# Graph attention on one core: another order of products in the first pair of tiles of a batch, and the mean's product one step later

## The chip, the cores and the metric

The kernel runs on one core of a Trainium2 chip. The metric is the device time of one execution in microseconds, the median of three runs. PE is the matrix engine, DVE the vector engine, ACT the scalar engine; POOL issues the indirect DMAs (gathers) and a few small operations, SP the plain DMAs.

## The reference, cut to what matters

`x` has 16 batches of 1024 nodes with 512 features, `adj` is one sparse 0/1 matrix of 1024 x 1024 for all batches, and there are 8 heads of 64.

```python
q = (x @ Wq + bq).reshape(b, n, H, HD)
k = (x @ Wk + bk).reshape(b, n, H, HD)
v = (x @ Wv + bv).reshape(b, n, H, HD)
scores = jnp.einsum('bqhd,bkhd->bhqk', q, k) / jnp.sqrt(jnp.float32(HD))
scores = scores + (1.0 - adj)[None, None, :, :] * -1000000000.0
attn = jax.nn.softmax(scores, axis=-1)
out = jnp.einsum('bhqk,bkhd->bqhd', attn, v).reshape(b, n, d)
return _layernorm(x + out @ Wo + bo)
```

## The kernel before

Nodes are ranked by their number of neighbours and cut into 8 tiles of 128 queries. The attention of a tile isn't a dense product: for each query, the rows k | v of its neighbours are fetched by gathers, one *block* at a time (a block is one neighbour for each of 128 queries). There are 530 blocks in all, 32 to 34 for a batch. A query without neighbours gets the average of all v, so each batch also needs that average as one more row of the table of k | v rows.

**The loop of steps.** The program is written out by one loop (L1485), with a step n for each block. A step puts into DVE's program the product q·k of block n + 4 (L1263), the sum of earlier blocks (L1307) and the scores (L1267); into ACT's the exponentials and the weighting of v (L1291); into POOL's the gathers of block n + 8. What earlier steps put off with `later(k, fn)` comes behind that (L1519), k steps after the call. Last come *units* of work for PE, out of two lists: `finishing` (the four products of an output tile with Wo, L1075) goes ahead of `fronts`. A step has a credit, a share of the work that is left, and hands out units as long as the credit is above zero; each unit takes its cost off (0.86 for a product, 0.44 for the transposes of one tile, 0.88 for the lone product). What a step hasn't used is carried over. If the next unit isn't ready yet, the loop breaks off. Functions on the list `urgent` are called behind the first unit of a step.

**The fronts** make q, k and v for all tiles, a pair of tiles (b, j) at a time, j from 0 to 3, as far as two batches ahead of the attention. For k and v together, a scheme with seven half-size products in place of eight is used (L984 to L996). Each unit holds two code products, which are four matmul instructions (a float32 product takes two). In its names, x and z are two fixed PSUM banks, used twice by each pair:

- x1 writes bank x; ACT copies it to e (L960); x2 adds to the same bank and may be handed out only when that copy is in the program. Then out_k copies the bank to k.
- p6 takes s2 as input, and DVE makes w out of it (L963); p7 takes s3, and DVE makes g (L966).
- z1 takes s1 and writes bank z; out_v1 on DVE (L975) makes v of the second tile out of it. z2 takes s4, adds to the same bank, may be handed out only when out_v1 is in the program, and waits for it on the chip. out_v0 (L979) follows z2.
- p4 makes k of the second tile (out_k1, L970).
- q0 and q1 are the products for q of the two tiles (L790), where they are needed.
- xt0 and xt1 transpose the two x tiles of the *next* pair (L748). One step later ACT copies the result (L752); one step after the second copy, `combine` (L774 to L777) makes s1 to s4 for the next pair on DVE. s1, s2 and s3 have one buffer each, s4 has two.

A unit of the seven is ready only when its pair's s1 to s4 are in the program:

```python
return [(2 * PRODUCT, pe, lambda: (need is None or need in R) and (b, j) in SX and bool(combined))]
```

In a first pair (j = 0) of a batch from 2 on, tile 1 needs no q, so q1 is empty. Tile 0 of an even and the following odd batch are treated together: in an even batch q0 is empty, in an odd one it is four products and the *lone product* (L881, in bf16), whose squares are summed on ACT (L889).

**The mean.** When both tiles of the last pair (j = 3) are sent, `add_v` (L854) adds their v to a running sum one step later, and one step behind that `mean_pe` (L856) is put on the urgent list: a product with a column of 1/1024 (L858). A step later ACT copies it (L862), SP stores it as the last row of the batch's table (L864), and `set_up[b]` is set. The gathers of the batch's blocks are only put into the program once that is set (L1504).

Of the kernel before, what the change touches and what calls it, by code (L numbers as in the profile page):

```python
# [177 lines left out]
def kernel(  # L178
# [75 lines left out]
    with ExitStack() as main:  # L254
# [6 lines left out]
        def fill_psum(name):  # L261
            return psum.tile([P, HALF], F32, tag="fill", name=name, bufs=4)
# [67 lines left out]
        def kv_of(b):  # L330

            if b < PAIRED_FROM:
                return solo_rows[b], 0
            rows = pair_views[b // 2 % 2][b % 2]
            return (rows, N + 1) if b % 2 else (rows[0:N + 1, :], 0)
# [104 lines left out]
        now, plan, rest, urgent, known, waiting, combined = [0], {}, {}, [], [], [], []  # L440

        def later(k, fn):
            plan.setdefault(now[0] + k, []).append(fn)
# [340 lines left out]
        def product(name, lhs, w, out):  # L784

            def unit(c):
                if c == 0:
                    PS[name] = fill_psum(name)
                p = PS[name]
                nc.tensor.matmul(p, lhs(c), w[:, c, :], start=(c == 0), stop=(c == NPAIR - 1))  # L790
                if c == NPAIR - 1:
                    del PS[name]
                    later(1, lambda: out(p))

            return [(PRODUCT, lambda c=c: unit(c), None) for c in range(NPAIR)]
# [11 lines left out]
        def pair(b, j):  # L807
# [8 lines left out]
            def out_q(i, p):  # L816

                assert gathered[0] >= start[max(0, b - ROWS + 1)]
                tag, bufs = ("q", 2) if b or j else ("y", Y_BUFS)
                q = work.tile([P, D], F32, tag=tag, name=f"q_{b}_{tt[i]}", bufs=bufs)  # L820
                nc.vector.scalar_tensor_tensor(q, p, scale, bq_bc, op0=OP.mult, op1=OP.add)
                later(1, lambda: nc.sync.dma_start(q_rows[b % ROWS][ds(tt[i] * P, P), :], q))

            def out_k(i, p):
                kv = new_kv(i)
                nc.scalar.copy(kv[:, 0:D], p)
                later_last(1, lambda: norm(b, tt[i], kv[:, 0:D]))

            def out_v(i, p):
                nc.scalar.copy(KV[b, tt[i]][:, D:], p)  # L830
                send(i)

            def send(i):
                assert b < PAIRED_FROM or gathered[0] >= start[max(0, b // 2 * 2 - 2)]
                kv = KV[b, tt[i]]
                rows, base = kv_of(b)
                for lo, hi in ((0, LONE), (LONE + P, 2 * P)) if b and tt[i] == 0 else ((tt[i] * P - (LONE if b and tt[i] == 1 else 0), None),):
                    hi = lo + P if hi is None else hi
                    part = slice(0 if lo % P == 0 or hi - lo == P else LONE, P if hi - lo == P or lo else LONE)
                    later(1, lambda lo=lo, hi=hi, part=part: nc.sync.dma_start(rows[base + lo:base + hi, :], kv[part, :]))  # L840
                R["sent"] = R.get("sent", 0) + 1
                if R["sent"] == 2:
                    later(1, add_v)
                    if j == NT // 2 - 1:
                        later(2, lambda: urgent.append(mean_pe))

            def add_v():
                kv = [KV.pop((b, t))[:, D:] for t in tt]
# [49 lines left out]
            def lhs(i):  # L898
                return lambda c: XT[b, tt[i]][:, ts(c, P)]

            q0, q1 = (
                product(f"pq_{b}_{tt[i]}", lhs(i), W["q"], lambda p, i=i: out_q(i, p)) if b == 0 or tt[i] != ONE_KEY else []
                for i in range(2)
            )
            if j == 0 and b >= PAIRED_FROM:
                q0 = []
                if merged(b):
                    q0 = product(f"pq_{b}_0", lambda c: BOTH[b // 2][:, 1, c, :], W["q"], lambda p: out_q(0, p))
                    q0 += lone_product()
            n = b * NT + 2 * j + 2  # L910
            xt = [u for t in (n, n + 1) if t < B * NT for u in transpose_x(t // NT, t % NT)]
# [24 lines left out]
            def a(i, h):  # L936
                return XT[b, tt[i]][:, ts(h, HD2)]

            def unit(bank, left, right, first, after, need):
                def pe():  # L940
                    if first:
                        R[bank] = fill_psum(f"p{bank}_{b}_{j}") if bank[0] == "p" else psum.tile(
                            [P, HALF], F32, tag=bank, name=f"{bank}_{b}_{j}", bufs=1
                        )
                    l = left()
                    for c in range(2):
                        nc.tensor.matmul(  # L947
                            R[bank], l[:, ts(c, P)], right[:, c, :], start=(first and c == 0), stop=(c == 1),
                            skip_group_check=True,
                        )  # L950
                    later(1, after)

                return [(2 * PRODUCT, pe, lambda: (need is None or need in R) and (b, j) in SX and bool(combined))]
# [14 lines left out]
            def out_k1():  # L968
                kv = KV[b, tt[1]]
                nc.vector.tensor_tensor(kv[:, 0:D], R["p4"], R["g"], op=OP.add)  # L970
                send(1)
                later_last(1, lambda: norm(b, tt[1], kv[:, 0:D]))
# [5 lines left out]
            def out_v0():  # L978
                nc.vector.tensor_tensor(KV[b, tt[0]][:, D:], R["z"], R["w"], op=OP.add)  # L979
                send(0)  # L980

            def s(i):
                return lambda: SX[b, j][i - 1]

            units = []
            units += unit("x", lambda: a(0, 0), B11, True, out_e, None)
            units += unit("p6", s(2), T2, True, out_w, None)
            units += q0
            units += unit("x", lambda: a(0, 1), B21, False, lambda: out_k(0, R["x"]), "e")
            units += unit("p7", s(3), T3, True, out_g, None)  # L990
# [472 lines left out]
        with tc.manual_schedule():  # L1463
# [3 lines left out]
            for b in range(B):  # L1467
                for j in range(NT // 2):
                    fronts += pair(b, j)
                fronts_by.append(sum(u[0] for u in fronts))  # L1470
# [14 lines left out]
            while n < total or plan or rest or urgent or done or finishing or spilled or lone_tiles or not guarded:  # L1485
# [6 lines left out]
                elif n in start:  # L1492

                    b = start.index(n)
# [110 lines left out]
```

## Time and profile before

| what | value |
|---|---|
| runs shown | 1876.87, 1874.72, 1875.09 us; median 1875.09 |
| profiled execution | 1894.52 us, of which the span of the profile is 1892.4 us |
| busy, of the span | PE 96%, DVE 90%, ACT 82%, POOL 67% |
| matmul instructions | 5149 |
| granted PE clock, mean | 0.990 |
| HBM traffic | 298 GB/s over the span |

A line of the busy table gives an engine's busy time, its share of the span and its instructions. A line of the groups gives code line, engine, operation, output and input tiles, shapes and count; then busy time and mean of one in ns; then the idle time of the engine just before the instructions and what ended most of it. A line of the waits gives who waited for whom, us in total, the number of times and the longest. A line of the timeline gives start, duration (a merged group's), engine, code line, operation, tiles, shapes and count, and in brackets idle time and its releaser; "issue" stands for a wait that the profile can't name. In the table of windows the columns are the stretch, its length, busy time and count of PE, PEld, DVE, ACT and POOL, the granted clock, the share of the DMA engines and GB/s.

### The profile page before, as it was taken

How to read it: one execution, taken by the hardware profiler on the slowest of the kernel's cores; microseconds unless marked ns; L12 is line 12 of the kernel's file. 1: busy time of each engine (PE TensorE's matmuls, PEld its weight loads, DVE VectorE, ACT ScalarE, POOL GpSimd, SP SyncE). 2: the span in 40 equal slices, each digit the busy share in tenths (PEclk: the TensorE clock that was granted, in tenths of full speed). 3: DMA queues.
4: the chain of work that ended last, by engine and by line, in shares of the span. 5: the costliest groups of instructions: out<-in, count | busy, mean ns of one | idle time of the engine just before them, and what ended most of it. 6: DMA issues, size and time to landing. Idle time of an engine off the chain costs nothing. (4 is left out here: it accounts for less than half of the span.)

```text
span 1892.4 us, 25171 instructions
## 1 busy us (share of the span) xinstructions
PE 1816.5 (96%) x5149; PEld 876.6 (46%) x5149; DVE 1695.3 (90%) x3470; ACT 1557.4 (82%) x6128; POOL 1262.6 (67%) x1189
## 2 busy tenths in 40 slices
PE   7979999999999999999999999999999999999996
PEld 3434444444545454444444444444545444444442
DVE  6888879999998999899999989899999989997875
ACT  3627868988888988988898878988899989977885
POOL 1366765777676776767676766767676866656884
PEclk9989999999999999999999999999999999999998
DMA  7356786888989897989889897989889899989993
GB/s 279 115 167 215 226 290 229 309 298 291 322 266 319 303 333 256 345 290 310 299 284 329 279 324 261 334 303 309 286 302 352 297 332 319 329 282 319 340 332 137
DMA packets 188149, 544.63 MB, mean 288 GB/s; under 512 B 32602, under 2 KB 32622, under 8 KB 187986
## 3 DMA queue, kind: packets, MB, share of 16 engines
q0 software_dynamic: 116400, 382.82, 60.4%
q1 hardware_dynamic: 68510, 154.30, 21.7%
q10 hardware_dynamic: 3076, 5.82, 0.8%
q14 instruction: 120, 0.98, 0.2%
q8 instruction: 43, 0.70, 0.2%
HBM read 419.52 MB, written 144.34 MB: 298 GB/s over the span
## 5 line engine op out<-in xcount | busy, mean ns | idle before, releaser
L1291 ACT ACTIVATE pv<-kvg,pv 128x64 f32<-128x64 f32 x3544 | 893.4, 340 | 1.8 <-issue 1.8
L1242 POOL DMA_INDIRECT kvg<-kv_pair,place_row x462 | 522.6, 1131 | 258.6 <-issue 94.5
L790 PE MATMUL po<-wo,oT 128*128 128x512 f32 x816 | 379.2, 600 | 2.0 <-DVE vsum L854 1.2
L790 PE MATMUL pq<-wq,xT 128*128 128x512 f32 x792 | 369.4, 598 | 1.3 <-DVE s L1267 0.8
L1267 DVE TENSOR_REDUCE s<-qk 128x8 f32<-128x512 f32 x530 | 360.8, 681 | 7.2
L1263 DVE TENSOR_TENSOR qk<-qt,kvg 128x512 f32<-128x512 f32 x434 | 296.8, 684 | 13.2 <-DMA kvg<-kv_pair,place_row 13.1
L947 PE MATMUL x<-b,xT 128*128 128x512 f32 x504 | 239.0, 597 | 0.1
L947 PE MATMUL pp<-t,s 128*128 128x512 f32 x504 | 237.3, 593 | 1.5 <-DVE t L383 1.5
L1307 DVE TENSOR_TENSOR pv<-pv,pv 128x520 f32<-128x520 f32 x329 | 228.4, 694 | 8.2 <-ACT pv L1291 8.0
L790 PEld LDWEIGHTS po<-wo,oT 128*128 128x128 f32 x816 | 153.4, 192 | 171.7 <-issue 162.7
L790 PEld LDWEIGHTS pq<-wq,xT 128*128 128x128 f32 x792 | 149.0, 192 | 169.3 <-issue 157.7
L1001 POOL DMA_INDIRECT x<-in_x_dram,asked_row x120 | 129.6, 1080 | 103.5 <-PE pxT L748 35.4
L1278 ACT ACTIVATE pv<-s,absent 128x8 f32<-128x8 f32 x434 | 126.8, 293 | 55.1 <-DVE s L1267 36.6
L1125 POOL DMA_INDIRECT out_dram<-y,asked_row x129 | 145.1, 1125 | 35.9 <-issue 25.0
L800 ACT ACTIVATE sq_k<-kv 128x128 bf16<-128x128 f32 x512 | 150.8, 300 | 8.4 <-DVE kv L970 4.5
L947 PEld LDWEIGHTS x<-b,xT 128*128 128x128 f32 x504 | 95.3, 192 | 111.6 <-issue 105.2
L947 PEld LDWEIGHTS pp<-t,s 128*128 128x128 f32 x504 | 94.1, 190 | 111.3 <-issue 102.2
L947 PE MATMUL z<-b,s 128*128 128x512 f32 x252 | 121.4, 604 | 13.1 <-DVE kv L975 10.4
L1196 POOL DMA_INDIRECT qg<-q_rows,query_row x96 | 105.5, 1099 | 28.5 <-issue 25.3
L1029 POOL DMA_INDIRECT y<-in_x_dram,asked_row x93 | 105.0, 1129 | 26.1 <-issue 25.8
L947 PE MATMUL z<-t,s 128*128 128x512 f32 x252 | 118.6, 593 | 0.0
L947 PE MATMUL pp<-t,xT 128*128 128x512 f32 x252 | 118.5, 592 | 0.0
(276 smaller groups left out, 2750.2 us busy)
## 6 DMA issues: line engine op xcount, KB each, us to landing
kv_pair<-kv SPq DMA_DIRECT2D x98, 512.0 KB
q_rows<-q SPq DMA_DIRECT2D x106, 256.0 KB
qt<-q_rows SPq DMA_DIRECT2D x98, 256.0 KB
residual<-x SPq DMA_DIRECT2D x36, 256.0 KB
y<-residual SPq DMA_DIRECT2D x36, 256.0 KB
kv_rows<-kv SPq DMA_DIRECT2D x15, 512.0 KB
kvg<-kv_pair,place_row POOLq DMA_INDIRECT x462
kv_pair<-kv SPq DMA_DIRECT2D x28, 256.0 KB
```

Source lines behind the costliest of these rows:

```text
L790: nc.tensor.matmul(p, lhs(c), w[:, c, :], start=(c == 0), stop=(c == NPAIR - 1))
L800: nc.scalar.activation(sq, s[:, ts(h, P)], AF.Square, scale=scale, accum_out=sums[:, h:h + 1])
L947: nc.tensor.matmul(R[bank], l[:, ts(c, P)], right[:, c, :], start=(first and c == 0), stop=(c == 1), skip_group_check=True,)
L1001: nc.gpsimd.indirect_dma_start(out=y, out_offset=None, in_=x_rows, in_offset=bass.IndirectOffsetOnAxis(ap=asked_row[:, t:t + 1], axis=0), ...
L1125: nc.gpsimd.indirect_dma_start(out=out_rows[b, t], out_offset=bass.IndirectOffsetOnAxis(ap=rows, axis=0), in_=y, in_offset=None, element_o ...
L1196: nc.gpsimd.indirect_dma_start(out=q, out_offset=None, in_=q_rows[b % ROWS], in_offset=bass.IndirectOffsetOnAxis(ap=rows, axis=0))
L1242: nc.gpsimd.indirect_dma_start(out=KG[n], out_offset=None, in_=rows, in_offset=bass.IndirectOffsetOnAxis(ap=(place_row if b else key_row)[ ...
L1263: nc.vector.tensor_tensor(QK[n], q, KG[n][:, 0:D], op=OP.mult)
L1267: nc.vector.tensor_reduce(S[n], QK.pop(n).rearrange("p (h d) -> p h d", d=HD), axis=AX.X, op=OP.add)
L1278: nc.scalar.activation(PV[n][:, D:], S.pop(n), AF.Exp, bias=bias)
L1291: nc.scalar.activation(pv[:, ts(h, HD)], v[:, ds(D + h * HD, HD)], AF.Copy, scale=pv[:, D + h:D + h + 1])
L1307: nc.vector.tensor_tensor(PV[b, t], PV[b, t], pv, op=OP.add)
```

## The change

In the first pair of a batch from 2 on, the list of units is put together in another order: the transposes of the next pair's first tile (xt0) take the place of q0 between p6 and x2; q0 (with the lone product) and the transposes of the second tile (xt1) take the place of q1 between z1 and p4. For all batches but the first, `mean_pe` is put on the urgent list one step later. Instructions, tiles and buffers stay the same.

```diff
                 if R["sent"] == 2:
                     later(1, add_v)
                     if j == NT // 2 - 1:
-                        later(2, lambda: urgent.append(mean_pe))
+                        later(3 if b else 2, lambda: urgent.append(mean_pe))
...
             units = []
             units += unit("x", lambda: a(0, 0), B11, True, out_e, None)
             units += unit("p6", s(2), T2, True, out_w, None)
+            if j == 0 and b > 1:
+                q0, q1, xt = xt[:1], q0 + xt[1:], []
             units += q0
             units += unit("x", lambda: a(0, 1), B21, False, lambda: out_k(0, R["x"]), "e")
             units += unit("p7", s(3), T3, True, out_g, None)
             units += xt
             units += unit("z", s(1), T1, True, out_v1, None)
             units += q1
             units += unit("p4", lambda: a(1, 1), T4, True, out_k1, None)
             units += unit("z", s(4), B22, False, out_v0, "v1")
             return units
```

## The prediction

> **What bounds the kernel now.** I read the page's busy table first, then the waits of PE, then the timeline around the longest of them.
>
> ```profile
> PE 1816.5 (96%) x5149; PEld 876.6 (46%) x5149; DVE 1695.3 (90%) x3470; ACT 1557.4 (82%) x6128; POOL 1262.6 (67%) x1189
> ...
> L947 PE MATMUL z<-b,s 128*128 128x512 f32 x252 | 121.4, 604 | 13.1 <-DVE kv L975 10.4
> ```
>
> PE is busy for 96% of the span. Away from its waits the timeline shows 8 matmuls in 3.43 us, one every 0.43 us without a gap, so a wait of PE that goes is worth its length, as long as no other engine sets the time of the next meeting point. The second product of bank z (z2) is the row that the change aims at.
>
> ```profile
> PE z L947 <- DVE kv L975: 10.4, 5, 3.9
> ...
> PE pm L858 <- DVE vsum L854: 2.7, 3, 1.2
> ```
>
> The timelines at the first pairs (j = 0) give the idle time before z2: batch 4 0.54 us, 6 1.23, 7 1.34, 8 2.67, 10 3.86, 11 0.83, 12 1.44, none in the others: 11.9 us. The mean's product (pm) waits in batches 2, 11, 14 and 15: 0.45 + 1.1 + 1.06 + 1.15 = 3.8 us (one of the four is put down to ACT). The longest wait, in batch 10:
>
> ```profile
> 1090.39 1.88 PE L947 MATMUL z<-t,s 128*128 128x512 f32 x4
> ...
> 1092.37 0.44 DVE L774 TENSOR_TENSOR s<-xT 128x256 f32<-128x256 f32 x1 [2.88 <-issue]
> ...
> 1097.11 0.68 DVE L975 TENSOR_TENSOR kv<-z,g 128x512 f32<-128x512 f32 x1
> ...
> 1097.85 2.61 PE L947 MATMUL z<-b,s 128*128 128x512 f32 x4 [3.86 <-DVE kv L975]
> ```
>
> DVE stands still for 2.88 us ahead of L774, the first sum of the next pair (combine). L774 overwrites s1, which has one buffer, and the first product of z (z1) reads s1: L774 starts 0.1 us after z1 ends. L975, which z2 needs, stands behind it.
>
> ```profile
> 1099.07:1102.48 3.41, 3.41 (x5) 1.35 (x4) 3.38 (x10) 0.21 (x1) 2.80 (x3) 0.50 0.84 273
> ```
>
> The seventh figure is the granted clock: half, for one stretch of 3.41 us after the wait. That costs another 1.7 us of PE.
>
> **Two rules of the Trainium skill.** "PSUM — Partial Sum Buffer", section "Engine vs sequencer instructions", says that VectorE's queue is strictly first in, first out. The 2.88 us above are that rule at work, and the forecast goes by it: what counts is where an instruction stands in DVE's program. "TensorE: Matmul & The Clock Gate", section "HAM oscillation", says that idle gaps of PE over about 3.4 us halve its clock. Here 3.86 us did; but in batch 8 a wait of 2.67 us was followed by 3.4 us at half clock as well. I go by the trace: a wait of some 2.7 us may cost 1.7 us more.
>
> **The change, part by part.** Units are dealt out by a loop whose steps are counted in the code; each step puts one product (L1263) into DVE's program, and units into PE's for as long as the credit is above 0. What a unit leaves to the other engines (later(1)) comes a step on, behind the product, sum and scores of that step: about 2 us of DVE (3 x 0.6 us, the spacing of DVE's rows). I followed the credit by hand through the fourteen first pairs, with the code's costs (0.86 a product, 0.44 a transposed tile, 0.88 the lone product).
>
> (a) *Order.* Even batches have no q0 and no q1 in this pair. Theirs becomes x1, p6, xt0, x2, p7, z1, xt1, p4, z2: between z1 and z2 there is only xt1 more, 4 transposes, 0.44 us, and z1 comes 0.44 us earlier. Odd batches get q0 (3.43 us), the lone product (0.9 us) and xt1 there. No unit is added or dropped. What has gone before z2 is the same set of units in both orders, so z2 keeps its step.
>
> (b) *z2.* Where z1 keeps its step, out_v1 keeps its place in DVE and the wait stays: batches 4, 6, 8 and 12 (5.9 us, and 1.7 us of clock in 8). In batch 7 z1 goes from step 183 to 181, z2 stays in 184: 1.3 us saved. In batch 10 z1 goes from 284 to 282 and z2 stays in 286; in 11 z2 likewise no longer waits.
>
> (c) *What is late next.* The next pair's first unit (x1') may only run two steps after xt1, when combine has been put into DVE's program. Moving xt1 behind z1 makes its step later: 16 instead of 15 in batch 2 (b2), 116 for 114 (b5), 252 for 250 (b9), 285 for 282 (b10), 320 for 319 (b11). In b2, b5, b10 and b11 x1' would be due one step too early; the loop breaks off and hands out no unit in that step. PE loses no instruction, but runs a step ahead, and the product after x1' (p6') reads s2, which combine writes. Batch 2 shows the price; PE, then DVE:
>
> ```profile
> 221.21 1.88 PE L947 MATMUL x<-b,xT 128*128 128x512 f32 x4
> 222.92 0.60 PE L1351 MATMUL poT<-ident,o 128*128 128x128 f32 x4
> 223.36 1.88 PE L947 MATMUL pp<-t,s 128*128 128x512 f32 x4
> ```
>
> ```profile
> 221.16 0.41 DVE L776 TENSOR_TENSOR s<-s,xT 128x256 f32<-128x256 f32 x1
> ...
> 222.55 0.68 DVE L979 TENSOR_TENSOR kv<-z,w 128x512 f32<-128x512 f32 x1
> ```
>
> s2 (L776) is there at 221.6, 1.8 us ahead of p6'. After the change combine stands one step later: behind L979, which can't start before z2 ends (221.4), and the next product, sum and scores. So 221.4 + 4 x 0.6 + 1.2 (L774 to L776) = 225.0, and p6' waits 225.0 - 223.36 = 1.6 us. The same sum gives 1.6 us in batch 5 and 0.6 in 9. In batch 11 DVE's sums held their place behind ACT (L1307 waits 0.70 us), so L774 moves from 1210.32 to behind L979 and one block without a sum: 1210.3 + 0.6 + 0.6 + 0.7 + 0.6 + 0.1 = 1212.9, s2 at 1214.0, and p6' starts then instead of at 1212.04: 2.0 us lost, the saved 0.83 included. In batch 10 DVE is rid of the 2.88 us and of combine (1.5 us of its time) ahead of L975; the scores of step 287 end at 1099.4 instead of 1103.8, s2 comes at 1100.5, and p6' starts then instead of at 1103.08: 2.6 us saved net, of the 3.86 + 1.7. These are estimates: the price of p6' lies between 0 (DVE makes it up) and some 2 us more than the sum says.
>
> (d) *pm one step later.* The wait for vsum goes. In batch 15 (1.1 us) and 2 (0.4) that is kept; in 11 DVE runs without a gap from pm to the wait of batch 12's z2, so PE only waits there instead: 0.
>
> (e) *What hangs on pm.* Behind it stand ACT's copy, SP's store of the mean, the flag set_up, and POOL's gathers of the batch's first rows. In batches 2 to 12 the gather follows pm by 20 us or more; in 13, 14 and 15 by 7.5 us. Batch 14, POOL, then DVE:
>
> ```profile
> 1630.80 1.05 POOL L1242 DMA_INDIRECT kvg<-kv_pair,place_row  x1 [4.47 <-DMA qt<-q_rows]
> ```
>
> ```profile
> 1635.90 0.69 DVE L1263 TENSOR_TENSOR qk<-qt,kvg 128x512 f32<-128x512 f32 x1 [1.57 <-DMA kvg<-kv_pair,place_row]
> ...
> 1639.67 0.69 DVE L1263 TENSOR_TENSOR qk<-qt,kvg 128x512 f32<-128x512 f32 x1 [0.91 <-DMA kvg<-kv_pair,place_row]
> ```
>
> ACT's copy moves from 1625.56 to the next step's, about 1628.1: 2.5 us. Store and gather follow, DVE waits 2.5 us longer, and at 1650.91 a transpose of PE starts 0.06 us after DVE's o, so there is no slack: 2.5 us lost, pm's own saving in this batch included. In 13 the next gathers are no later than now (two come in one step, and a gather of x gets ahead of them); in 15 DVE waits for PE three times (1.21, 0.64, 1.56 us) and has room: 0 each, bound 2.5 us each.
>
> (f) q0's rows are stored some steps later, on SP; the batch's first step is over 30 steps off: nothing. The lone squares of ACT (16 instructions, 1.7 us) move with phat; ACT is 82% busy: nothing.
>
> Sum, savings positive: z2 and p6' 1.3 (b7) + 2.6 (b10) - 2.0 (b11) - 1.6 (b2) - 1.6 (b5) - 0.6 (b9) = -1.9; pm 1.1 + 0.4 = 1.5; gathers -2.5. In all 2.9 us slower. The profiled execution took 1894.5 us (span 1892.4), 19 us over the median of 1875.1; I carry the difference over: 1878.0 us.
>
> **Rivals.**
> *Faster: p6' doesn't wait.* DVE may reach combine sooner than its spacing before suggests, since L975 is out of its way. Then b7, b10 and b11 give 6.0 + 1.7 and pm 2.6 us (b11's counted), less 2.5: 7.8 us, 1867. For it: DVE has waits of its own at z1 (6.0 us in 10). Against it: L979 can't start before z2 ends.
> *Faster still:* the even batches' waits go too, because 0.44 us shift the two engines against each other: another 7.6 us, 1860.
> *Slower: the mean's row is late in all three last batches.* If the gathers of 13 and 15 also delay DVE by 2.5 us each, 5 us are added, and 1.7 us if p6' of batch 11 waits long enough for half clock: 2.9 + 5 + 1.7 = 9.6 us, 1885. It decides as soon as the first gather takes over 4 us to land; in batch 14 it took 5.1 us.
> *It doesn't do what it says:* in even batches hardly any work comes between; that is in the forecast, and if the odd ones don't gain either, z2's 1.3 + 2.6 us go: 1882, within the range.
>
> **Chances.** About 0.2% (3.7 us) is what a measurement of this kernel can tell from no change. My forecast, inside that band: 0.36. p6' not waiting: 0.26; faster still: 0.06. Late mean: 0.32. The band alone reaches from 1871.4 to 1878.8; with both main rivals and some us for the bounds of (c) and (e) the range is 1864 to 1888, which leaves out the fourth case and tails.
>
> **What would show it.** No idle time before z2 in batches 7, 10 and 11, and none of half clock near batch 10; the waits of 4, 6 and 12 still there; a new row "pp waits for DVE s" (L776), near 1.6 us each, in 2, 5 and 11; no wait of pm for vsum; longer waits of qk for kvg at the start of batch 14. Wrong: if that row is missing, or if the even batches' waits go with the odd ones'.

## The result, and the profile after

The changed kernel took 1882.92 us (median of 16 runs, 1876.77 to 1886.13), the kernel before on the same chip 1875.91 us (16 runs, 1874.72 to 1883.73). The ratio, taken over all these runs, is 1.003, with a 95% interval of 1.0021 to 1.0039: 5.6 us slower (the two medians lie 7.0 us apart), just beyond the 0.2% that a measurement can tell.

The two profiled executions can't be subtracted: that of the kernel before lay 19 us above its own runs, and the changed kernel's profile (1882.43 us, span 1880.6) leads it by 6 us at block 40, ahead of nearly all that the change touches. So I compare waits and stretches, not spans.

From the page of the changed kernel (lines from 988 on have moved by 2; 14 records of matmuls are missing from this trace, x5135 for 5149, and PEld shows that none was dropped):

```profile
PE 1812.8 (96%) x5135; PEld 876.7 (47%) x5149; DVE 1696.6 (90%) x3470; ACT 1555.3 (83%) x6128; POOL 1262.1 (67%) x1189
...
L947 PE MATMUL pp<-t,s 128*128 128x512 f32 x504 | 239.6, 598 | 8.8 <-DVE s L776 7.0
...
L947 PE MATMUL z<-b,s 128*128 128x512 f32 x252 | 119.0, 595 | 4.7 <-DVE kv L975 4.5
L947 PE MATMUL pp<-t,xT 128*128 128x512 f32 x252 | 119.0, 594 | 3.2 <-DVE q L821 2.5
```

The idle time ahead of z2 (the row z) has gone from 13.1 to 4.7 us. Two rows have come: p6 and p7 (input s) wait 8.8 us, mostly for L776, and p4 (input xT) waits 3.2 us. The waits of PE in the same kernel:

```profile
PE pp L947 <- DVE s L776: 7.0, 3, 4.6
...
PE z L947 <- DVE kv L975: 4.5, 4, 2.6
PE pp L947 <- DVE q L821: 2.5, 2, 1.5
```

No wait of the mean's product for vsum is left.

**Batch 2, p6' late.** The timelines of the changed kernel, PE and then DVE:

```profile
218.25 1.88 PE L947 MATMUL x<-b,xT 128*128 128x512 f32 x4
221.77 1.95 PE L947 MATMUL pp<-t,s 128*128 128x512 f32 x4 [1.63 <-ACT y L1123]
```

```profile
218.02 0.69 DVE L979 TENSOR_TENSOR kv<-z,w 128x512 f32<-128x512 f32 x1 [0.81 <-PE z L947]
...
220.49 0.46 DVE L774 TENSOR_TENSOR s<-xT 128x256 f32<-128x256 f32 x1
220.88 0.41 DVE L775 TENSOR_TENSOR s<-xT,xT 128x256 f32<-128x256 f32 x1
221.21 0.41 DVE L776 TENSOR_TENSOR s<-s,xT 128x256 f32<-128x256 f32 x1
```

Combine stands behind L979 and a step's product, sum and scores, as worked out ahead of the run; L776 ends at 221.62 and p6' starts at 221.77. The bracket names ACT's y, which p6' doesn't read: among several waits the profile names the one it saw last. In batches 5, 9 and 10 it names L776 itself.

**Batch 10.** PE, DVE, and the table of windows of the changed kernel:

```profile
1085.09 0.60 PE L1353 MATMUL poT<-ident,o 128*128 128x128 f32 x4
1090.27 3.75 PE L947 MATMUL pp<-t,s 128*128 128x512 f32 x4 [4.58 <-DVE s L776]
```

```profile
1089.71 0.41 DVE L776 TENSOR_TENSOR s<-s,xT 128x256 f32<-128x256 f32 x1
```

```profile
1087.80:1091.20 3.40, 0.93 (x1) 0.50 (x2) 3.37 (x9) 3.40 (x17) 2.79 (x3) 0.50 1.05 353
1091.20:1094.60 3.40, 3.40 (x5) 1.35 (x4) 2.34 (x4) 1.34 (x6) 2.49 (x4) 0.50 0.92 325
```

z2's 3.86 us are gone, but p6' waits 4.58 us. It then runs at half clock: 3.75 us for four matmuls, not 1.88.

**Batch 13, p4 late.** This I had not foreseen. PE, then DVE:

```profile
1399.41 3.60 PE L790 MATMUL pq<-wq,both 128*128 128x512 f32 x8
1402.84 1.06 PE L881 MATMUL phat<-wq,both 128*128 128x512 bf16 x3
1403.75 0.60 PE L1353 MATMUL poT<-ident,o 128*128 128x128 f32 x4
1404.18 0.60 PE L748 MATMUL pxT<-ident,x 128*128 128x128 f32 x4
1405.72 1.98 PE L947 MATMUL pp<-t,xT 128*128 128x512 f32 x4 [0.94 <-DVE q L821]
```

```profile
1404.99 0.68 DVE L821 SCALAR_TENSOR_TENSOR q<-pq,bq_bc 128x512 f32<-128x512 f32 x1
```

p4 reads the transposed x and a weight, nothing that L821 writes. What they share is PSUM: q's product, the lone product, the transposes and p4 all take their banks from one tag with four buffers (`fill`, L262). q0 now stands close ahead of p4: with a transpose of the output (poT) in between, p4 is the fourth to take a bank after q, so by the code it gets q's own, which DVE empties a step later.

**Stretches.** To separate the change from disturbances elsewhere I took, out of the timelines, the time from the first matmul of x1 in a batch's first pair to the first of p6', in four profiles in which that batch has the old order (before, its repeat, the mean late up to 12, and the order in the other half of the batches) and four in which it has the new one (after, its repeat, the order alone, and the order in this half); the runs are told of below. Of batch 2 each side leaves out one value that is 6 to 9 us longer. Where the wait of a single place is given from here on, it is the spacing of PE's matmuls less the usual one (0.43 us behind a product, 0.11 behind a transpose), some 0.15 us above the brackets.

| batch | old order, us | new order, us | mean difference | forecast |
|---|---|---|---|---|
| 2 | 19.58 to 19.63 | 21.29 to 21.57 | +1.8 | +1.6 |
| 5 | 31.22 to 31.27 | 32.98 to 33.03 | +1.7 | +1.6 |
| 7 | 29.98 to 30.78 | 28.71 to 30.48 | -0.7 | -1.3 |
| 8 | 25.00 to 29.45 | 24.93 to 30.42 | -0.7 | 0 |
| 9 | 28.28 to 28.88 | 29.23 to 35.66 | +3.3 | +0.6 |
| 10 | 27.87 to 29.18 | 25.63 to 25.69 | -2.6 | -2.6 |
| 11 | 26.02 to 26.62 | 26.45 to 33.14 | +2.6 | +2.0 |
| 13 | 27.46 to 29.02 | 28.65 to 32.71 | +3.1 | 0 |
| 15 | 33.35 to 33.61 | 34.87 to 35.63 | +1.9 | 0 |

All even batches together come to -3.0 us, all odd ones to +11.8 us. In 9, 11 and 13 the new order doesn't only add time, it adds spread. That holds for 7 too: in the two profiles with its new order that aren't in the table, it took 34.8 and 34.4 us.

The first profile of the changed kernel is the quiet one, as told below. Set against the least of the four old values in each of the fourteen batches, it is 5.3 us longer in sum: 1.8 us each in 2 and 5, 2.0 in 15, 1.2 in 13, 1.0 in 9 and 0.4 in 11, less 2.2 in 10 and 0.7 in 7.

### The profile page after: what moved, and what is told of

Same layout as the page of the kernel before. It is cut to its first block, busy times and chain, and to the rows that moved or that the text cites. A ratio compares the mean times of both kernels' runs of the same rounds, so it can differ in the third digit from the quotient of the medians.

```text
span 1880.6 us, 25156 instructions
## 1 busy us (share of the span) xinstructions
PE 1812.8 (96%) x5135; PEld 876.7 (47%) x5149; DVE 1696.6 (90%) x3470; ACT 1555.3 (83%) x6128; POOL 1262.1 (67%) x1189
## 5 line engine op out<-in xcount | busy, mean ns | idle before, releaser
L1265 DVE TENSOR_TENSOR qk<-qt,kvg 128x512 f32<-128x512 f32 x434 | 297.1, 685 | 16.8 <-DMA kvg<-kv_pair,place_row 16.4
L1123 ACT ACTIVATE y<-y,stats 128x512 f32<-128x512 f32 (+1 forms) x129 | 103.4, 807 | 18.9 <-DVE stats L1118 17.8
```

Source lines behind the costliest of these rows:

```text
L1265: nc.vector.tensor_tensor(QK[n], q, KG[n][:, 0:D], op=OP.mult)
```

## The experiments

My theory at the start was the prediction's: the order costs where combine, and so p6', comes a step late. The rival was that the late mean costs. Three sets of four kernels were run, in the order of this section, each set beside the kernel before on a chip of its own. Its median there was 1895.4, 1911.4 and 1908.2 us, so only ratios are compared, and those of different sets with care.

**The kernel before, again** (no edit).

> The kernel before, unchanged, as a second look. Both theories: 1876 us, ratio 1.000 within 0.1%. Its first profiled execution lay 19 us over the median and already 6 us behind that of the changed kernel before the first changed pair mattered, so a second profile shows which of the waits of PE belong to the kernel. Expected: the waits of z2 for out_v1 in batches 4, 6, 7, 10, 11 and 12 again, that of batch 8 (2.67 us, with half clock) gone, a span of 1874 to 1880 us.

Ratio 0.9997 (0.9981 to 1.0013), and the waits of z2 come back: 0.9 us in batch 6, 1.5 in 7, 2.9 in 8, 4.0 in 10, 1.6 in 12. They belong to the program, not to one execution; that of batch 8, which I had expected to go, too.

**The order alone.**

```diff
-                        later(3 if b else 2, lambda: urgent.append(mean_pe))
+                        later(2, lambda: urgent.append(mean_pe))
```

> The new order of units alone, the mean's product where it was. Theory O (the order costs: p6' waits for combine in batches 2, 5, 9 and 10, some 9 us and 3 us of half clock, against 12 us of z2 saved, and p4 waits 3 us): 2 to 4 us slower than before, 1879. Theory M (the mean's delay costs all of it, the order gains): 2 to 6 us faster than before, 1871.

Ratio 1.0053 (1.0033 to 1.0074): 10 us, no less than the whole change costs. p6' waits in the same batches (1.65, 1.76, 1.60 and 4.68 us in 2, 5, 9 and 10), and p4 for 3.4 and 2.3 us in 13 and 15. z2 in 8, which waited 2.8 us before, waits 3.8.

**The mean alone.**

```diff
-                        later(2, lambda: urgent.append(mean_pe))
+                        later(3 if b else 2, lambda: urgent.append(mean_pe))
```

> The mean's product one step later alone, the old order. Theory O (the order carries the loss): within 2 us of before, since 1.5 us of waits saved and 2.5 us of late gathers nearly cancel: 1877. Theory M (the late first rows of batches 13 to 15 carry it): 5 to 8 us slower, 1882, with waits of qk for kvg at the starts of 13, 14 and 15 longer by 2 us each.

Ratio 1.0018 (1.0005 to 1.003): 3.4 us, the smaller part. z2 of batch 12 waits 3.5 us here and 1.6 in the repeat of before: what pm no longer waits in 11 is only put off. At the starts of batches 13, 14 and 15 the products wait 6.6 us in all, mostly for gathers, where before and its repeat show 5.9 and 2.5. p6' of batch 6 waits 2.4 us, with half clock behind it; I hadn't forecast that.

**Combine a step sooner**, in the step of ACT's copy, for tile 3 of a batch.

```diff
-                        later(1, combine)
+                        if b > 1 and t == 3:
+                            combine()
+                        else:
+                            later(1, combine)
```

> The changed kernel, but in the pairs concerned combine is put into DVE's program in the same step as ACT's copy of the second transposed tile, one step sooner, so that x1' isn't held back. Theory O: the rows 'pp waits for DVE s L776' (7.0 us in three, and half clock near 1090) go nearly all, 7 to 11 us less than the changed kernel: 1873. Theory M: no more than 2 us less, 1881.

Ratio 1.0031 (1.001 to 1.0052): no gain that shows. p6' no longer waits in 5 and 9, and the stretch of batch 5 is back at 31.23 us: there the late combine is the cause. But it waits 3.6 us in 2 and 2.1 in 10. Combine now stands in the same step as the copy it reads, and DVE waits there twice as often. The waits of DVE, in the repeat of before and then in this kernel (L777 is its first line of combine):

```profile
DVE s L774 <- ACT xT L752: 3.5, 3, 1.6
```

```profile
DVE s L777 <- ACT xT L752: 8.7, 6, 3.9
```

From DVE the wait goes on to PE: in 11, p6' waits 5.1 us behind the longest of them. That one isn't the doing of the edit alone, since ACT stood still ahead of the copy itself:

```profile
1209.80 0.59 ACT L752 COPY xT<-pxT 128x512 f32<-128x512 f32 x1 [4.46 <-remote]
```

**xt1 ahead of z1**, the mean at its old place; only q0 goes behind z1.

```diff
-                q0, q1, xt = xt[:1], q0 + xt[1:], []
+                q0, q1, xt = xt[:1], q0, xt[1:]
```

> The new order without its late part, and the mean's product where it was: xt0 between p6 and x2, xt1 still ahead of z1, q0 with the lone product behind z1. Theory O (the order costs because combine comes a step later and because p4 takes the PSUM buffer of a q just made): p6' in 2, 5, 9 and 10 doesn't wait, the waits of p4 for q (batches 13 and 15) shrink, z2 doesn't wait in 7 and 11; the waits of z2 in 4, 6, 8, 10 and 12 are those of before. 2 to 3 us faster than before, ratio 0.999. Rival (it's q0 coming late, or xt0 coming early, that costs): as slow as the order alone, ratio 1.004 or more.

Ratio 1.0013 (0.9994 to 1.0033), not to be told from no loss, and not the gain of 0.1% that I expected. p6' waits in one batch only (6, 1.8 us), and the stretch of batch 5 is 31.23 us again; p4 still waits 1.9 us in 13. z2 of batch 10 waits 4.1 us again, since z1 isn't any earlier.

**The mean late only up to batch 12**, in the old order.

```diff
-                        later(2, lambda: urgent.append(mean_pe))
+                        later(3 if 0 < b < 13 else 2, lambda: urgent.append(mean_pe))
```

> The old order; the mean's product one step later only in batches 1 to 12, where the gathers of the first rows follow it by 20 us or more. If the delay costs through the late first rows of 13 to 15: ratio 1.000, within 0.1%. If it costs otherwise (the longer way of the stored mean, other places of the product in PE's program): 1.002 as for the delay in all batches.

Ratio 1.001 (0.9988 to 1.0032): unclear, between nothing and the 1.0018 of the late mean in all batches. It doesn't settle how much of that lies in 13 to 15.

**The order alone, not in 2, 5, 9 and 10**, the batches with the forecast waits of p6'.

```diff
-            if j == 0 and b > 1:
+            if j == 0 and b > 1 and b not in (2, 5, 9, 10):
```

> The new order alone, but not in batches 2, 5, 9 and 10, in which p6' waited for combine (1.7, 1.8, 1.6 and 4.7 us in the profile of the order alone, with half clock after the last). Theory O: ratio between that of before and that of the order alone: 1.002, since the waits of p4 (3.4 us in 13, 2.3 in 15) stay, 2.4 us of z2 are saved in 7 and 11, and batch 10 has its old wait of 4.0 us again. Rival (p6' waits are made up later): 1.005, the order alone.

Ratio 1.0041 (1.0022 to 1.006), against 1.0053. My theory in its narrow form falls here: without the four batches a loss of at least 0.2% is left. p4 waits in 13 and 15 (3.1 and 2.3 us), p6' in 11 (5.1 us).

**The changed kernel again**, on that chip.

> The changed kernel, unchanged, beside the others on their chip: ratio 1.003 to 1.007 (order alone 1.0053 and mean alone 1.0018 on a slower chip, 1.003 for both on the first). The same waits as in its first profile: p6' for s2 in 2, 5, 9 and 10, p4 in 3, 13 and 15, z2 in 12.

Ratio 1.0061 (1.0036 to 1.0086). The loss is real, and here rather larger; p6' waits 4.7 us in 10 once more, and p4 3.2 and 1.6 us in 13 and 15. p6' now waits 3.9 us in 9 and 6.4 in 11 as well.

**The order in odd batches alone, and in even ones alone.**

```diff
-            if j == 0 and b > 1:
+            if j == 0 and b > 1 and b % 2:
```

> The order in odd batches alone, the mean at its old place. My theory (the loss is made of waits in the first pairs: p6' for s2 where xt1's step is later, and p4 for a buffer of the tag that the products for q fill just ahead of it): z2's waits go in 7 and 11 (2.5 us gained), p6' waits in 5, 9 and 11 (about 4 us), p4 in 13 and 15 (5.7 us) and x2 in 13 (1 us), with one stretch of half clock in 13 (1.7 us): 10 us lost, ratio 1.004 to 1.005. Rival (each reordered first pair costs alike, whatever waits it shows, because the engines lose their tuned distance): half of the 0.53% of the order alone, 1.0027, and as much in the even batches.

> The order in even batches alone, the mean at its old place. My theory: p6' waits in 2 and 10 (1.7 and 4.7 us), z2 no longer in 10 (4.0 us gained) and as before in 4, 6 and 12, no wait of p4: 2 us lost, ratio 1.000 to 1.002. Rival: 1.0027.

(The second has `b % 2 == 0`.) Odd: 1.0108 (1.007 to 1.0145), 20 us. Even: 0.9981 (0.9961 to 1.0), 3.6 us faster, if anything. The signs are those of the table of stretches, with the odd side larger. The rival of an equal price for each reordered pair is out.

Batch 9 of the first of them shows one way in which the spread arises. ACT, DVE and PE:

```profile
989.75 0.20 ACT L889 ACTIVATION_READ_ACCUMULATOR sq_hat<-phat 128x1 f32 x1 [0.50 <-issue]
991.23 0.22 ACT L889 ACTIVATE sq_hat<-phat 128x64 bf16<-128x64 f32 x1 [1.27 <-ACT sq_hat L889]
...
992.68 0.23 ACT L889 ACTIVATE sq_hat<-phat 128x64 bf16<-128x64 f32 x1 [0.94 <-ACT sq_hat L889]
...
994.14 0.22 ACT L889 ACTIVATE sq_hat<-phat 128x64 bf16<-128x64 f32 x1 [0.93 <-ACT sq_hat L889]
```

```profile
995.59 0.16 DVE L894 TENSOR_REDUCE lone_hat<-hat 128x1 f32<-128x8 f32 x1 [4.48 <-ACT pv L1280]
...
1000.59 0.42 DVE L776 TENSOR_TENSOR s<-s,xT 128x256 f32<-128x256 f32 x1
```

```profile
1001.15 3.75 PE L947 MATMUL pp<-t,s 128*128 128x512 f32 x4 [7.27 <-DVE s L776]
```

The lone squares take 6.4 us here, and in nearly all other places 1.7. DVE's L894, which reduces them, stands ahead of combine and holds it 4.5 us; p6' waits 7.3. In the order alone the squares of batch 9 took 1.7 us, L894 waited 0.3 and p6' 1.6. Stretched squares are also found in batches with the old order (2.6 us in 13 of the kernel before, 4.4 in 13 of the even batches alone), so the order needn't have made them. What it does is put the squares, L894 and combine close together in front of p6', with nothing between to absorb a delay. With xt1 ahead of z1, L894 waited 3.6 us in batch 9 (squares of 4.8 us), and the stretch was 28.4 us, as in the old order.

In 11 and 13 the squares never took over 1.8 us in the new order. There DVE stands still elsewhere. Batch 11 of the changed kernel's repeat, PE and then DVE:

```profile
1212.12 1.88 PE L947 MATMUL pp<-t,xT 128*128 128x512 f32 x4
...
1225.57 3.61 PE L947 MATMUL pp<-t,s 128*128 128x512 f32 x4 [6.19 <-DVE s L776]
```

```profile
1221.64 0.69 DVE L970 TENSOR_TENSOR kv<-pp,g 128x512 f32<-128x512 f32 x1 [3.77 <-remote]
...
1225.10 0.42 DVE L776 TENSOR_TENSOR s<-s,xT 128x256 f32<-128x256 f32 x1
```

L970 reads p4, whose matmuls ended at 1214.0 by the profile; the trace gives it no wait but that for PE. Yet it starts 7.6 us later, and combine stands behind it ("remote": the profile finds no instruction that ended near the release). The same befalls L970 in 11 with the order not in 2, 5, 9 and 10 (5.7 us idle, 7.3 after p4) and L821 in 9 of this repeat (3.1 us idle, 4.5 after q). Such waits come with the old order too, at less cost: in batch 9 of the even batches alone L975 stood 5.4 us, and the stretch was 28.9 us against 28.3; in the changed kernel's repeat, with L821 late, it was 32.2 against 29.2 in its first profile. Between 200 and 1750 us, 13 of the 14 profiles have 4 to 18 waits of DVE and ACT marked "remote". The first profile of the changed kernel has none. Why PE's results are taken up late isn't shown.

**p4 ahead of q0**, in the order alone: z1, p4, q0, xt1, z2, to keep p4 from the banks of q.

```diff
-            units += q1
+            if j:
+                units += q1
             units += unit("p4", lambda: a(1, 1), T4, True, out_k1, None)
+            if not j:
+                units += q1
```

> The order alone, but with p4 ahead of q0, the lone product and xt1, so that in odd batches no product for q stands between z1 and p4; the mean at its old place. My theory: p4 and x2 hardly wait any more (6.7 us and the half clock of batch 13 gained against the order alone), z2 and p6' as with the order alone: ratio 1.000 to 1.002. Rival (p4's waits are only where a lag between the engines happens to show; the next product that needs a buffer waits instead): the wait is found at another product and the ratio stays at 1.004 to 1.006.

Ratio 1.0136 (1.0098 to 1.0175), the slowest of all. The rival was right that the wait turns up at another product, and the loss is beyond what either expected. p4 waits no more, but xt1 is later still, and the waits of PE in this kernel read:

```profile
PE pp L947 <- DVE s L776: 16.8, 8, 4.7
...
PE pp L947 <- DVE s L775: 2.8, 1, 2.8
```

These are eight waits of 16.8 us in all, where the order alone has four of 9.0. p6' waits in even batches too: 4 (2.5 us) and 14 (2.6 us), where only xt1 comes behind p4.

**The order in batches 7 and 8 alone.**

```diff
-            if j == 0 and b > 1:
+            if j == 0 and b in (7, 8):
```

> The order in batches 7 and 8 alone, where the trace of the changed kernel shows less waiting than the one before; the mean at its old place. My theory: z2's wait in 7 goes (1.5 us), that in 8 shrinks by 2 us, perhaps with its half clock (1.7 us), and nothing comes instead: 1.5 to 5 us gained, ratio 0.997 to 0.999, the only version of these that would be faster than both. Rival: two of fourteen reordered pairs lose their share, 1.0008.

Ratio 0.9997 (0.9974 to 1.0019). z2 waits neither in 7 nor in 8, but 7's stretch took 34.4 us, with the lone squares stretched to 4.4 us and L970 standing still for 5.3. A gain of 3 us is not excluded; none is shown. No version here is shown to beat the kernel before; the even batches alone come nearest.

**Together.** Three versions differ mainly in where xt1 stands. Ahead of z1, p6' waits 1.8 us in all and the ratio is 1.0013. Behind z1 and q0: 10.3 us, 1.0053. Behind z1, p4 and q0: 21.6 us, 1.0136. That a later xt1 makes p6' wait is shown. That the whole time follows it is not shown: the three ratios come from three chips, and on the third's chip the order in odd batches alone, with xt1 as in the second, came to 1.0108, which the intervals don't tell from 1.0136.

## Why the prediction was right or wrong

It said 2.9 us slower, and 5.6 us were measured. The mechanism, a late combine that p6' waits for, was right; some terms of the sum were mis-sized, and one was missing. That the total came so near is partly luck. The forecast put the order at 1.9 us and the mean at 1.0; on another chip they cost 10 and 3.4 us alone, and on a third the whole change cost 11.7.

**(a), (b) z2.** Right for 7, 10 and 11: no wait is left there. The waits of 4, 6 and 12 stayed (0.74, 0.89 and 2.79 us). Batch 8 was to keep its 2.7 us and half clock; it kept 0.75 and full clock in the changed kernel. But its stretch was 30.4 us in the order alone, with a wait of 3.8 us, and 25.0 with the order in odd batches only, where batch 8 isn't reordered, so this gain hangs on what comes before it. The wait in 8 is of the late kind told of above: L975 itself stood 2.0 us in the kernel before and 3.4 in the order alone, marked "remote".

**(c) p6'.** In batches 2, 5 and 10 the working held within 0.3 us of the means, in three first pairs that differ. "None of half clock near batch 10" was wrong: the sum for p6' left out that its own wait, 4.6 us, is long enough for half clock, and two stretches of it followed; 1.9 us of them lie in p6' itself and eat most of the 2.6. In 11 the changed kernel's stretch was no longer than before (26.45 against 26.58 us), in its repeat 33.1, behind the late L970; the forecast of 2.0 fits neither. In 9 it was 0.95 us longer, near the forecast, but 3.3 in the mean. The single timeline I worked from had no disturbance in 9 and 11, and my sum had no term for one.

**(d) pm.** Right: its waits went, and that of batch 11 came back as 1.2 us more at z2 of 12.

**(e) Gathers.** Near in sum, wrong in place. I put 2.5 us on batch 14 and nothing on 15. The first products of 13, 14 and 15 together waited 6.7 us in the changed kernel and 7.0 in its repeat (3.4 of these without a releaser that the profile could name), against 5.9 and 2.5 in the kernel before and its repeat: 2.7 us more in the mean, but the repeats differ by more than that. Batch 14 waited 2.5 us in both first profiles; 15 waited 1.4 and 1.1 us where it had not waited before. The slower rival, 5 us more from 13 and 15, did not occur.

**(f) "q0's rows ... nothing", "the lone squares of ACT ... nothing".** The first "nothing" is the step that failed. I asked whether q0's rows are needed soon, not which buffers its products hold: p4 waits for one, 3.7 us in 3, 13 and 15 in the changed kernel, 5.8 in its repeat, 5.7 in the order alone. The second held in both profiles of the changed kernel, where L894 waits 0.3 us at most, and failed in batch 9 of the odd batches alone. I had asked whether ACT has room, not what is queued behind L894 on DVE. The Trainium skill, "PSUM — Partial Sum Buffer", section "Engine vs sequencer instructions", has the rule that I cited for combine and should have applied here: VectorE's queue is strictly first in, first out, so L894, waiting 4.48 us, holds everything behind it. This trace agrees.

**Rivals.** "p6' doesn't wait" fell: with the whole new order it waits in every profile, in at least two of 2, 5 and 10. "Faster still" did not occur: with the order in the even batches alone, z2 still waits 0.7, 0.9 and 1.6 us in 4, 6 and 12, and the 3.6 us measured there have an interval that touches zero.

**Open.** The odd batches alone measured 20 us, the odd stretches in the table add up to 11.8; the rest isn't placed. Its profiled execution, at 1919.1 us, was the fastest of its six and lay only 11 us above the median of the kernel before. Nor is it shown why ACT's squares are stretched and PE's results taken up late now and then. Whether a second buffer for s1 to s3 would take the price from p6' was not tried.

## What to carry to other kernels

When filler work is put between a producer and its consumer, look at what the filler was ahead of: here transposes that were filler for z2 are the head of the next pair's chain, and p6' waited longer with each unit put in front of them (1.8, 10.3, 21.6 us). For every moved unit, list the PSUM buffers it takes from a shared tag and the instructions it queues on the other engines, with what stands behind those. And where an order leaves an engine without slack, cost it from several executions: a quiet trace doesn't show what a delay will cost.

## What the runs showed of the hardware

- **Half clock after waits below 3 us, but not always.** The Trainium skill's "TensorE: Matmul & The Clock Gate", section "HAM oscillation", names gaps over about 3.4 us. Here the clock was halved after a wait of p6' of 2.2 us (by the bracket) in the late mean alone (batch 6), and after one of 2.5 us with p4 ahead (batch 14), but not after one of 3.3 us of z2 in batch 12 of the late mean alone. What decides between these isn't shown.
- **The same 16 instructions of ACT take 1.7 us or up to 6.4.** In 14 profiles there are 98 groups of lone squares; 10 took 2.5 us or more, with gaps of 0.2 to 1.4 us between a few of them, most of them put down to ACT's own earlier square. They lie in batches 7, 9, 13 and 15, in old and new orders.
- **A product of PE can be taken up late by an engine that stands idle.** L970 started 7.6 us after p4 had ended, as the profile models it, with 3.77 us of idle time (batch 11 of the changed kernel's repeat). 13 of 14 profiles have such waits, of either order.
- **The kernel before itself took 1876, 1911, 1895 and 1908 us** (medians) on four occasions, with spreads of 9 to 24 us; 0.3% could only be told by runs side by side on one chip.
